# A four-layer graph network on one core: when the rows of layer 0 are gathered, released and written

## The chip, the cores and the metric

The kernel runs on one core of a Trainium2 chip. The metric is the device time of one execution in microseconds (us), lower is better; each kernel is run several times and the median counts. The engines are named as in the profile: PE is TensorE's matmul, PEld its weight load, DVE VectorE, ACT ScalarE, POOL GpSimd, SP SyncE. L849 is line 849 of the kernel before.

## The reference

A graph of 3125 nodes and 100,000 edges goes through four layers. Each layer ends in `x = layernorm(x + layer(x))`. Layer 0, the one that the change touches, is an attention over the edges that end in a node:

```python
pre_edge = hP1[dst] + hP2[src] + zP3[edge_type]          # 128 wide
logit_edge = leaky(pre_edge) @ y_w                       # 8 heads
alpha = softmax of the logits over the edges of each dst (and one self edge)
t_edge = hWh[src] + zWz[edge_type]
out = leaky(segment_sum(alpha * t_edge, dst) + residual_weight * h)
# nodes without edges keep h
```

`h` is the input x, `z` a table of 500 relations with 64 values each. Layer 1 averages the rows of the neighbours and applies two dense layers. Layer 2 is an attention with four heads and a bias from edge attributes; layer 3 an attention whose matrices depend on node type and edge type. Layers 1 to 3 use the same edges.

## The kernel before

The nodes are ordered by their number of edges and cut into 25 tiles of 128 (`NT`, `P`). A node is a partition. Tile t has CAP[t] slots, and slot s holds the s-th edge of each of its 128 nodes: 57 slots in the largest tile, 21 in the smallest, 821 in all. Eight slots (`W`) make a chunk, four a group. There are 215 groups.

At the start, tables are built in HBM: `h_tab` has, for each node, the 264 values of the source's part of an edge (`HC`), `z_tab` the same for a relation, with the relation's own 64 values. Layer 0 then runs over the tiles (L1026). For a tile it gathers the tile's own rows of x (`own`, L799 to L803, a memset and an indirect gather, three buffers of `x`), multiplies them by the weights (`prologue`, which leaves `hw` and `hq`), and walks over the tile's chunks. The function `runs` (L70) cuts a tile into runs of at most three chunks and says of each chunk in which of two ways it is done:

- `gathered` (L851): for each slot POOL gathers 128 rows of `h_tab` into `hs` and 128 rows of `z_tab` into `zs`; DVE adds them.
- `multiplied` (L871): POOL gathers only `hs`; the relation's part comes from matmuls. SP loads the relation numbers as `rb` (L878), DVE makes one-hot matrices `oh` (L883), PE multiplies them by the table into `zps` (L892), ACT copies that to `zT` (L894), PE adds it to `pre` (L896) and into `t_ps` (L904), which DVE adds to `hs` (L905). 77 chunks are done so.

In both, PE forms `pre` for each group of four slots, ACT takes its relu as `low` (L831), and PE multiplies `low` by the heads' weights into `lg` (L835). After the relu of group g, ACT copies one value of it into `gates[g]` (L833).

`gates` holds POOL back. `held(rows, g)` (L846 to L849) lets POOL copy `gates[g - LEAD]`, with LEAD = 6, into the first partition of the rows that the following gathers fill. The copy has to wait for ACT's copy of six groups earlier, and the gathers follow it on POOL. `hs` has eight buffers, a chunk each. In `gathered` there is one such copy for each four slots; in `multiplied` one for a whole chunk, ahead of its eight gathers:

```python
hs = wp.tile([P, W, HC], F32, name="hs", bufs=8)
held(hs, g)
for s in range(n):
    gather(hs[:, s, :], h_tab, srcx[:, o + s:o + s + 1])
```

After a run, the softmax weights and the weighted sums of its chunks are put on the list `owed`, and after the last run of a tile `close` (L953) is put there too. The list is paid bit by bit (`pay_some`) between the chunks of the next run, so a tile is closed in the first run of the next tile. `close` forms the layer's output `y` (L1000, which reads the tile's `x`), its layernorm `x1` (L759 is the layernorm's last instruction), and scatters the 128 rows of `x1` to the table `x1_tab` in HBM with `put` (an indirect DMA of POOL, L106). Layer 1 loads that table.

The prologue of tile t+1 stands ahead of tile t's last chunk, `own(t + 1)` at the start of tile t. Work for later layers (counts of edges by pairs, names beginning with `c_`) is woven between the chunks by the generator `steps`.

The order of the instructions on each engine is not quite that of the source. The program is recorded and a planner writes out each engine's list by costs and due times that it assumes, with `tc.high_priority` bringing some instructions forward. So an instruction of a tile can stand on its engine among those of its neighbours: the scatter of tile 5's rows, for example, is issued by POOL during tile 7.[...]

Of the kernel before, what the change touches and what calls it, by code (L numbers as in the profile page):

```python
# [8 lines left out]
F32 = mybir.dt.float32  # L9
# [9 lines left out]
P = 128  # L19
N = 3125  # L20
NT = 25
# [7 lines left out]
D = 128  # L29
# [59 lines left out]
def tile_gnn(ctx, tc, a, out):  # L89
# [12 lines left out]
    def gather(dst, table, idx, **kw):  # L102
        return G.indirect_dma_start(out=dst, out_offset=None, in_=table, in_offset=indirect(idx), **kw)  # L103
# [373 lines left out]
    od = Order("d", order_d)  # L477
# [300 lines left out]
    with tc.tile_pool(name="l0", bufs=2) as wp, tc.tile_pool(name="l0s", bufs=1) as sp, \  # L778
# [67 lines left out]
        def held(rows, g):  # L846

            if g is not None and g >= LEAD:
                G.tensor_copy(rows[:1, :, 0], gates[:1, g - LEAD:g - LEAD + 1].to_broadcast([1, rows.shape[1]]))  # L849
# [21 lines left out]
        def multiplied(hq, o, n, zbT, first, lg_ps, g):  # L871

            hs = wp.tile([P, W, HC], F32, name="hs", bufs=8)
            held(hs, g)
            for s in range(n):
                gather(hs[:, s, :], h_tab, srcx[:, o + s:o + s + 1])
            rb = wp.tile([P, W * P], F16, name="rb")
            nc.sync.dma_start(rb[:, :n * P], rel_tab[o:o + n].rearrange("(o s) p -> o (s p)", o=1)  # L878
                              .to_broadcast([P, n * P]))
            ohs = []  # L880
            for i in range(NK):
                oh = wp.tile([P, W * P], BF16, name="oh", bufs=NK + 2)
                V.tensor_scalar(oh[:, :n * P], rb[:, :n * P], relid[:, i:i + 1], None, op0=OP.is_equal)  # L883
                ohs.append(oh)
            zT = wp.tile([P, W * P], F32, name="zT")
            for s0 in range(0, n, 4):
                k = min(4, n - s0)
                cols = slice(s0 * P, (s0 + k) * P)
                zps = ps1.tile([P, 4 * P], F32, name="zps")[:, :k * P]
                for i in range(NK):  # L890
                    for k2 in range(2):
                        T.matmul(zps, zq[:, i, 2 * R * k2:2 * R * (k2 + 1)], ohs[i][:, cols], start=(i + k2 == 0),  # L892
                                 stop=(i == NK - 1 and k2 == 1))
                A.activation(zT[:, cols], zps, AF.Copy)  # L894
                pre = argument(hq, k)
                T.matmul(pre[:, :k], zw[:, :D], zT[:, cols], start=False, stop=False)  # L896
                for s in range(k):
                    T.matmul(pre[:, s, :], hs[:, s0 + s, :D], ident, start=False, stop=(s == k - 1))  # L898
                logits(pre, k, lg_ps[:, s0:s0 + k], g + s0 // 4)
            for s0 in range(0, n, 3):  # L900
                k = min(3, n - s0)
                t_ps = ps1.tile([P, 3, HC - D], F32, name="t_ps")
                for s in range(k):
                    T.matmul(t_ps[:, s, :], zT[:, (s0 + s) * P:(s0 + s + 1) * P], zw[:, D:], start=True, stop=True)  # L904
                V.tensor_add(hs[:, s0:s0 + k, D:], hs[:, s0:s0 + k, D:], t_ps[:, :k])  # L905
            assert n == W
            zh = wp.tile([P, W // 2, P], F32, name="zh", bufs=1)
            z3 = zT.rearrange("z (s p) -> z s p", p=P)
            V.tensor_add(zh, z3[:, :W // 2], z3[:, W // 2:])
            halved(zh, W // 2, zbT if first else None)  # L910
            if not first:
                V.tensor_add(zbT, zbT, zh[:, 0])
            return hs
# [39 lines left out]
        def close(t, x, hw, ac, za, zbT):  # L953

            zaT_ps = ps1.tile([P, P], F32, name="tp", tag="misc")
            T.transpose(zaT_ps[:R], za, ident)
            zaT = wp.tile([R, P], F32, name="zaT")
            A.activation(zaT, zaT_ps[:R], AF.Copy)
            zb_ps = ps1.tile([P, 2 * D], F32, name="zb_ps", tag="misc")
            T.matmul(zb_ps, zbT, zw[:, :2 * D], start=True, stop=False)  # L960
            T.matmul(zb_ps, zaT, zw[:R, :2 * D], start=False, stop=True)
            zb = wp.tile([P, 2 * D], F32, name="zb")
            V.tensor_scalar(zb, zb_ps, od.rdeg[:, t:t + 1], None, op0=OP.mult)
            self_ = wp.tile([P, 2 * D], F32, name="self")
            V.tensor_add(self_, hw[:, D:3 * D], zb)
            V.tensor_add(self_[:, :D], self_[:, :D], hw[:, :D])
            V.scalar_tensor_tensor(self_[:, :D], self_[:, :D], 0.2, self_[:, :D], op0=OP.mult, op1=OP.max)
            sT = transposed(wp, ps1, self_[:, :D], "xT", "misc")
            sl_ps = ps1.tile([P, H], F32, name="sl_ps", tag="misc")
            T.matmul(sl_ps, sT, yw, start=True, stop=True)  # L970

            sl = wp.tile([P, H], F32, name="sl")
            V.tensor_sub(sl, sl_ps, hw[:, D + HC:])
            mf = wp.tile([P, 3, H], F32, name="mf")
            V.tensor_max(mf[:, 0, :], sl, m[:, t, :])
            V.tensor_sub(mf[:, 1, :], sl, mf[:, 0, :])
            V.tensor_sub(mf[:, 2, :], m[:, t, :], mf[:, 0, :])
            A.activation(mf[:, 1:, :], mf[:, 1:, :], AF.Exp)
            V.tensor_mul(l[:, t, :], l[:, t, :], mf[:, 2, :])
            V.tensor_add(l[:, t, :], l[:, t, :], mf[:, 1, :])  # L980
            rl = wp.tile([P, H], F32, name="rcl")
            V.reciprocal(rl, l[:, t, :])
            V.tensor_mul(mf[:, 1:, :], mf[:, 1:, :], rl.unsqueeze(1).to_broadcast([P, 2, H]))

            def heads(ap):
                return ap.rearrange("p (h d) -> p h d", h=H)

            ts = self_[:, D:]
            V.tensor_mul(heads(ac), heads(ac), mf[:, 2, :].unsqueeze(2).to_broadcast([P, H, D // H]))
            V.tensor_mul(heads(ts), heads(ts), mf[:, 1, :].unsqueeze(2).to_broadcast([P, H, D // H]))  # L990
            V.tensor_add(ac, ac, ts)
            V.scalar_tensor_tensor(ac, x, rw, ac, op0=OP.mult, op1=OP.add)
            V.scalar_tensor_tensor(ac, ac, 0.2, ac, op0=OP.mult, op1=OP.max)
            has = wp.tile([P, 2], F32, name="has")
            V.tensor_scalar(has[:, 0:1], od.deg[:, t:t + 1], 0.0, None, op0=OP.is_gt)
            V.tensor_scalar(has[:, 1:2], od.deg[:, t:t + 1], 0.0, 1.0, op0=OP.is_le, op1=OP.add)

            V.tensor_scalar(ac, ac, has[:, 0:1], None, op0=OP.mult)
            y = wp.tile([P, D], F32, name="y")
            V.scalar_tensor_tensor(y, x, has[:, 1:2], ac, op0=OP.mult, op1=OP.add)  # L1000
            x1 = wp.tile([P, D], F32, name="x1")
            layernorm(wp, x1, y, t)
            put(x1_tab, od, t, x1)

            x1T = transposed(wp, ps1, x1, "xT", "misc")
            u_ps = ps1.tile([P, D], F32, name="u_ps", tag="misc")
            T.matmul(u_ps, x1T, w1T, start=True, stop=True)
            u3 = wp.tile([P, 3, D], BF16, name="u3")
            A.activation(u3[:, 0, :], u_ps, AF.Copy)
            rest = wp.tile([P, D], F32, name="rest")  # L1010
            V.tensor_sub(rest, u_ps, u3[:, 0, :])
            V.tensor_copy(u3[:, 1, :], rest)
            V.tensor_sub(u3[:, 2, :], rest, u3[:, 1, :])
            nc.sync.dma_start(u_tab[:, t * 3 * D:(t + 1) * 3 * D], u3.rearrange("p k d -> p (k d)"))

        x1st = own(0)
        ahead = x1st, prologue(0, x1st)
        owed = []
        g = 0

        def pay_some(parts):
# [4 lines left out]
        for t in range(NT):  # L1026
            n = CAP[t]
            x, (hw, hq) = ahead
            if t + 1 < NT:
                x_next = own(t + 1)  # L1030
            ac, za, _ = sums_of(t)
            lg_ps = ps1.tile([P, max(CAP), H], F32, name="lg")
            zbT = wp.tile([P, P], F32, name="zbT")
            unset = True
            for run in runs(t):
                hss = []
                for i, (s0, w, mult) in enumerate(run):
                    o = OFF[t] + s0
                    if s0 + w == n and t + 1 < NT:

                        ahead = x_next, prologue(t + 1, x_next)
                    if mult:
                        hs = multiplied(hq, o, w, zbT, unset, lg_ps[:, s0:s0 + w], g)
                        unset = False
                    else:
                        hs = gathered(hq, lambda s: srcx[:, o + s:o + s + 1], rel[:, o:o + w], w, za,
                                      lg_ps[:, s0:s0 + w], g)
                    g += -(-w // 4)
                    hss.append((s0 - run[0][0], w, hs))
                    pay_some(len(run) - i if len(runs(t)) > 1 else max(1, len(run) - 1 - i))  # L1050

# [12 lines left out]
                    owed.append(lambda ac=ac, hs=hs, lg=lg, q=q, w=w: spread(ac, hs, lg[:, q:q + w], w))  # L1064
            owed.append(lambda t=t, x=x, hw=hw, ac=ac, za=za, zbT=zbT: close(t, x, hw, ac, za, zbT))
        pay_some(1)


    with ExitStack() as ctx1, tc.tile_pool(name="l1", bufs=2) as wp, tc.tile_pool(name="l1s", bufs=1) as sp:
# [371 lines left out]
```

## Time and profile before

| | |
|---|---|
| time, median of 3 runs | 5285.81 us (5254.62 to 5292.59) |
| profiled execution | 5243.0 us |
| its span in the profile | 5241.3 us |
| layer 0 | about 208 to 2490 us of the span |
| layer 1 | 2490 to 2620 us |
| layer 2 | 2620 to 3900 us |
| layer 3 | 3900 to 5241 us |
| PE, DVE, POOL busy | 41%, 58%, 55% of the span |

The profile is one execution; its instructions' times are measured by the chip's profiler. The borders of the layers are read from where the lines of each begin and end. Busy time is a sum over instructions of an engine. A "group" is all instructions of one line and operation: its busy time, the mean of one in ns, and the idle time of the engine just before them with the work that ended most of it. The "waits" view sums that idle time by the waiting instruction and its releaser. POOL issues the indirect DMAs[...].

### The profile page before, as it was taken

How to read it: one execution, taken by the hardware profiler on the slowest of the kernel's cores; microseconds unless marked ns; L12 is line 12 of the kernel's file. 1: busy time of each engine (PE TensorE's matmuls, PEld its weight loads, DVE VectorE, ACT ScalarE, POOL GpSimd, SP SyncE). 2: the span in 40 equal slices, each digit the busy share in tenths (PEclk: the TensorE clock that was granted, in tenths of full speed). 3: DMA queues.
4: the chain of work that ended last, by engine and by line, in shares of the span. 5: the costliest groups of instructions: out<-in, count | busy, mean ns of one | idle time of the engine just before them, and what ended most of it. 6: DMA issues, size and time to landing. Idle time of an engine off the chain costs nothing. (4 is left out here: it accounts for less than half of the span.)

```text
span 5241.3 us, 41048 instructions
## 1 busy us (share of the span) xinstructions
PE 2170.7 (41%) x12091; PEld 1405.0 (27%) x12091; DVE 3025.1 (58%) x7369; ACT 1018.4 (19%) x2777; POOL 2860.7 (55%) x3030
## 2 busy tenths in 40 slices
PE   7267676677767677777830122222232000000000
PEld 5145444455545454545310001011111000000000
DVE  8346555666656666656224576556664554454646
ACT  1023233333333333332100111111111000000000
POOL 0545444555545454453047666666663777666664
PEclk9578778778877787878865555555566555555555
DMA  3423222333323233332533333333342333233232
GB/s 82 122 80 86 80 80 80 87 99 90 99 79 87 75 90 86 82 97 75 215 106 99 99 109 106 109 105 113 104 113 73 105 96 93 79 92 94 86 92 58
DMA packets 213060, 498.45 MB, mean 95 GB/s; under 512 B 62329, under 2 KB 109100, under 8 KB 208185
## 3 DMA queue, kind: packets, MB, share of 16 engines
q0 software_dynamic: 136448, 397.65, 26.8%
q1 hardware_dynamic: 76344, 97.76, 6.0%
q8 instruction: 102, 1.67, 0.1%
q14 instruction: 166, 1.36, 0.1%
HBM read 424.65 MB, written 70.63 MB: 94 GB/s over the span
## 5 line engine op out<-in xcount | busy, mean ns | idle before, releaser
L103 POOL DMA_INDIRECT kv<-kv_tab,pay_sb x821 | 783.2, 954 | 384.9 <-issue 245.6
L103 POOL DMA_INDIRECT hs<-h_tab,srcx x821 | 848.3, 1033 | 262.0 <-issue 212.9
L103 POOL DMA_INDIRECT kv<-ktv_tab,pay_sb x821 | 802.6, 978 | 333.0 <-issue 244.2
L730 DVE TENSOR_REDUCE u<-msg 128x128 f32<-128x1024 f32 (+4 forms) x228 | 384.0, 1684 | 144.4 <-remote 94.6
L892 PE MATMUL zps<-oh,zq 128*128 128x512 bf16 x1232 | 397.4, 443 | 37.1 <-DVE oh L883 20.7
L835 PE MATMUL lg<-yw,low 128*128 128x8 f32 x1642 | 242.0, 274 | 150.0 <-ACT low L831 72.7
L849 POOL COPY hs<-gates 1x8 f32<-1x8 f32 (+3 forms) x133 | 41.2, 310 | 467.0 <-ACT gates L833 446.6
L835 PEld LDWEIGHTS lg<-yw,low 128*128 128x128 f32 x1642 | 234.5, 218 | 210.3 <-ACT low L831 100.1
L103 POOL DMA_INDIRECT zs<-z_tab,rel x205 | 213.1, 1039 | 124.7 <-issue 55.2
L623 ACT ACTIVATE c_oha<-c_oha,srclo 128x50 bf16<-128x50 bf16 (+2 forms) x821 | 206.0, 345 | 264.9 <-DVE c_oha L571 193.0
L904 PE MATMUL t_ps<-zw,zT 128*128 128x136 f32 x1232 | 225.7, 312 | 75.2 <-DVE hs L905 36.4
L905 DVE TENSOR_TENSOR hs<-hs,t_ps 128x408 f32<-128x408 f32 (+1 forms) x231 | 122.0, 528 | 227.8 <-PE t_ps L904 81.3
L726 DVE TENSOR_TENSOR msg<-kv,ex 128x1024 f32<-128x1024 f32 (+4 forms) x228 | 248.7, 1102 | 2.9 <-issue 1.8
L896 PE MATMUL pre<-zT,zw 128*128 128x512 f32 x308 | 205.7, 756 | 101.6 <-issue 62.4
L741 PE MATMUL tp<-ident,an 128*128 128x128 f32 x25 | 11.3, 453 | 560.7 <-DMA kv<-kv_tab,pay_sb 172.0
L904 PEld LDWEIGHTS t_ps<-zw,zT 128*128 128x128 f32 x1232 | 194.5, 213 | 109.7 <-issue 50.0
L898 PEld LDWEIGHTS pre<-ident,hs 128*128 128x128 f32 x1232 | 189.0, 221 | 95.3 <-issue 94.6
L824 PE MATMUL pre<-identb,hq 128*128 128x512 bf16 (+3 forms) x645 | 204.6, 417 | 5.9 <-issue 3.4
L831 ACT ACTIVATE low<-pre 128x512 f32<-128x512 f32 (+2 forms) x215 | 122.9, 574 | 400.8 <-PE pre L898 159.1
L1290 PE MATMUL xk_ps<-of,xqb 128*128 128x512 f32 x50 | 50.9, 1121 | 358.0 <-DVE xqb L759 204.9
L898 PE MATMUL pre<-ident,hs 128*128 128x128 f32 x1232 | 194.1, 306 | 0.0
L1378 DVE TENSOR_TENSOR qk<-kv,qp 128x1024 f32<-128x1024 f32 (+4 forms) x114 | 126.5, 1110 | 114.9 <-DMA kv<-ktv_tab,pay_sb 98.2
(399 smaller groups left out, 5384.6 us busy)
## 6 DMA issues: line engine op xcount, KB each, us to landing
rb<-rel_tab SPq DMA_DIRECT2D x77, 256.0 KB
c_tab<-c_sb SPq DMA_DIRECT2D x25, 768.0 KB
cs<-c_tab SPq DMA_DIRECT2D x6, 3200.0 KB
hs<-h_tab,srcx POOLq DMA_INDIRECT x821
kv<-kv_tab,pay_sb POOLq DMA_INDIRECT x821
kv<-ktv_tab,pay_sb POOLq DMA_INDIRECT x821
h_tab<-h SPq DMA_DIRECT2D x25, 132.0 KB
zs<-z_tab,rel POOLq DMA_INDIRECT x205
```

What stands on the lines that cost most here:

```text
L103: return G.indirect_dma_start(out=dst, out_offset=None, in_=table, in_offset=indirect(idx), **kw)
L623: A.activation(oha[:, s // 2, 0, :, s % 2], oha[:, s // 2, 1, :, s % 2], AF.Copy, scale=srclo[:, o:o + 1])
L726: V.tensor_tensor(msg[:, :n, :].rearrange("p s (h d) -> p s h d", h=heads), val.rearrange("p s (h d) -> p s h d", h=heads), ex.unsqueeze(3 ...
L730: V.tensor_reduce(u, msg[:, :n, :].rearrange("p s d -> p d s"), AX.X, OP.add)
L824: T.matmul(pre[:, :k], hq[:, i, :], identb.unsqueeze(1).to_broadcast([P, k, P]), start=(i == 0), stop=False)
L831: A.activation(low[:, :k], pre[:, :k], AF.Relu)
L835: T.matmul(lg_ps[:, s, :], low[:, s, :], yw8, start=True, stop=True)
L892: T.matmul(zps, zq[:, i, 2 * R * k2:2 * R * (k2 + 1)], ohs[i][:, cols], start=(i + k2 == 0), stop=(i == NK - 1 and k2 == 1))
L896: T.matmul(pre[:, :k], zw[:, :D], zT[:, cols], start=False, stop=False)
L898: T.matmul(pre[:, s, :], hs[:, s0 + s, :D], ident, start=False, stop=(s == k - 1))
L904: T.matmul(t_ps[:, s, :], zT[:, (s0 + s) * P:(s0 + s + 1) * P], zw[:, D:], start=True, stop=True)
L1378: V.tensor_mul(qk[:, :n], kv[:, :n, :D], qp.unsqueeze(1).to_broadcast([P, n, D]))
```

## The change

There are three edits, all in layer 0.

1. In `multiplied` a gate copy stands ahead of each four gathers instead of ahead of all eight. The second four wait for the gate of the next group.
2. `own(t + 1)` moves from the start of tile t to just ahead of its last chunk, beside the prologue that uses it.
3. `close` no longer scatters the tile's `x1`; it appends it to the list `finished`. After each chunk of a tile's last run `put_rows(1)` scatters what is in the list but for the newest entry, so that tile t-2's rows leave in tile t's last run. After the last tile `put_rows(0)` scatters the rest. `x1` gets three buffers.

```diff
@@ def multiplied
             hs = wp.tile([P, W, HC], F32, name="hs", bufs=8)
-            held(hs, g)
             for s in range(n):
+                if s % 4 == 0:
+                    held(hs[:, s:min(s + 4, n)], g + s // 4)
                 gather(hs[:, s, :], h_tab, srcx[:, o + s:o + s + 1])
@@ def close
-            x1 = wp.tile([P, D], F32, name="x1")
+            x1 = wp.tile([P, D], F32, name="x1", bufs=3)
             layernorm(wp, x1, y, t)
-            put(x1_tab, od, t, x1)
+            finished.append((t, x1))
@@ ahead of the loop over the tiles
-        owed = []
+        owed, finished = [], []
+
+        def put_rows(keep):
+
+            while len(finished) > keep:
+                k, rows = finished.pop(0)
+                put(x1_tab, od, k, rows)
+
@@ for t in range(NT)
             x, (hw, hq) = ahead
-            if t + 1 < NT:
-                x_next = own(t + 1)
             ac, za, _ = sums_of(t)
...
-            for run in runs(t):
+            runs_t = runs(t)
+            for run in runs_t:
                 hss = []
                 for i, (s0, w, mult) in enumerate(run):
                     o = OFF[t] + s0
                     if s0 + w == n and t + 1 < NT:
 
+                        x_next = own(t + 1)
                         ahead = x_next, prologue(t + 1, x_next)
...
                     g += -(-w // 4)
+                    if run is runs_t[-1]:
+                        put_rows(1)
                     hss.append((s0 - run[0][0], w, hs))
...
         pay_some(1)
+        put_rows(0)
```

## Prediction

> **What bounds the kernel now.** I read the busy shares first, then busy time by stage, then the waits of POOL and of PE inside layer 0, then the timeline around the waits that the change touches. The first line is the span; the second the engines' busy time; then the row of the gate copies (columns: busy, mean ns | idle time before it, and what ended most of that).
>
> ```profile
> span 5241.3 us, 41048 instructions
> ...
> PE 2170.7 (41%) x12091; PEld 1405.0 (27%) x12091; DVE 3025.1 (58%) x7369; ACT 1018.4 (19%) x2777; POOL 2860.7 (55%) x3030
> ...
> L849 POOL COPY hs<-gates 1x8 f32<-1x8 f32 (+3 forms) x133 | 41.2, 310 | 467.0 <-ACT gates L833 446.6
> ```
>
> No engine is full over the span, so I cut it by layers (columns: window, its length, busy PE, PEld, DVE, ACT, POOL, clock, DMA share, GB/s): layer 0, then layer 1, layer 2, layer 3.
>
> ```profile
> 208.00:2490.00 2282.00, 1613.89 (x9845) 1114.50 (x9844) 1382.57 (x3954) 747.17 (x2119) 1162.85 (x1231) 0.78 0.32 86
> 2490.00:2620.00 130.00, 105.23 (x440) 46.77 (x441) 33.79 (x148) 14.66 (x52) 2.77 (x1) 0.88 0.58 216
> 2620.00:3900.00 1280.00, 302.68 (x719) 139.13 (x716) 733.12 (x1596) 157.67 (x359) 811.91 (x851) 0.58 0.35 107
> 3900.00:5241.00 1341.00, 41.91 (x89) 18.50 (x87) 715.76 (x1191) 76.46 (x171) 847.81 (x867) 0.51 0.30 87
> ```
>
> The change touches layer 0 alone. There PE is busy 1613.9 of 2282 us (71%), POOL 51%: PE is nearest to a bound. What does POOL wait for in that window (total, times, longest)?
>
> ```profile
> POOL hs L849 <- ACT gates L833: 446.6, 66, 38.6
> ...
> POOL x L801 <- DVE y L1000: 139.7, 12, 18.7
> POOL x_tab L106 <- DVE x L759: 79.6, 11, 27.1
> ```
>
> The first wait is wanted: the gate keeps POOL six groups behind PE's use. The other two are what the moves aim at. Are gathers late? I took, from the trace's instructions, each gather's end and the matmul that reads its slot: the smallest distance is 25 us, the median 59. So gathers are not late, and a wait of POOL as such costs PE nothing. What costs is something else. There are stretches of layer 0 in which PE, PEld, DVE and ACT have no instruction at all while POOL gathers without a pause:
>
> ```profile
> 233.20:257.80 24.60, 0.00 (x0) 0.00 (x0) 0.00 (x0) 0.00 (x0) 18.69 (x21) 0.50 0.47 126
> 887.40:899.60 12.20, 0.00 (x0) 0.00 (x0) 0.00 (x0) 0.00 (x0) 6.87 (x8) 0.63 0.35 95
> ```
>
> I call them holds. Together the four engines stand still 318 us in layer 0, in 86 pieces over 1 us and many short ones; 243 us lie under gathers. Most end 1 to 4 us after the run of gathers ends. In the second, POOL's last gather starts at 895.46 and DVE and ACT move again from 899.70:
>
> ```profile
> 895.46 0.94 POOL L103 DMA_INDIRECT hs<-h_tab,srcx  x1 [0.30 <-issue]
> 899.70 0.26 DVE L571 TENSOR_TENSOR c_oha<-c_digb,c_up 128x200 bf16<-128x200 bf16 x1 [20.65 <-remote]
> ...
> 901.43 0.58 ACT L831 ACTIVATE low<-pre 128x512 f32<-128x512 f32 x1
> ```
>
> PE's semaphore updates for matmuls that ended from 881.8 on arrive bunched at 899.6. So long unbroken runs of gathers go with engines that hear of each other late. I counted, for each gather, how many came before it since POOL's last other instruction or pause over 1 us, with the still time of all four beside it: 1st to 4th: 572 gathers, 0.15 us each (85.7); 5th to 8th: 337, 0.353 (119.0); 9th to 12th: 113, 0.517 (58.4); later: 52, 0.914 (47.5). The sum is 310.6 us.
>
> [...]
>
> **The change part by part.**
> (1) A second gate in each of the 77 multiplied chunks. 154 of the 215 groups are in them; 76 gates are new (133 to 209; the very first chunks have none). A copy between two gathers takes 0.19 us and lengthens the pause from 0.30 to 0.45 us: 0.34 us each, 76 x 0.34 = 26 us of POOL, hidden in its 446.6 us of gate waits. The added wait: behind it on POOL's queue stand the other four gathers, then the next chunk. The gate of group g-5 opens on average 10.8 us after that of g-6 (median 6.5, 90% within 25.7); I replayed POOL's list with these times: the later four gathers move by a median of 2.5 us, 75% by at most 9.1, at most 26.5; median distance to the reader falls from 59 to 53, the smallest stays near 23. Gate waits grow by some 157 us in the replay, off the path. So by readiness of data it costs nothing. If that cover is gone, every us beyond 23 is paid by PE.
> What it can bring: no run of multiplied gathers is longer than four without another POOL instruction. If a copy alone starts the count anew, counts become 841, 135, 32, 18 (gathers and scatters of rows among them), and the still time 841 x 0.15 + 135 x 0.353 + 32 x 0.517 + 18 x 0.914 = 126 + 48 + 17 + 16 = 207, with 7 for the row transfers 214: 96 us less than 310. If only a real pause counts, the replay gives nothing (239 to 250 in its measure). A gate that makes POOL wait is a pause; one already open is only a copy. In seven places a hold ended 1 to 3 us after a copy in mid-run, some 0.7 endings per us against 0.2 elsewhere: few, but for the first reading. I take two thirds of the 96, 64: not all, as seven cases are few.
> (2) Own rows gathered at the last chunk. Memset and gather (0.20 + 1.02 us) remain, 25 of each; they pass the tile's earlier gathers on POOL, and SP is not involved. The 12 waits (139.7 us) for y of two tiles back go: y is done by then. But the gate after them is late next: in 10 of 12 POOL waits again there, as here, where 18.63 us at x are followed by 6.20 at the gate.
>
> ```profile
> 1032.79 0.20 POOL L801 MEMSET x<- 128x128 f32 x1 [18.63 <-DVE y L1000]
> 1033.61 1.02 POOL L103 DMA_INDIRECT x<-in_x,node_d  x1 [0.61 <-POOL x L801]
> 1040.83 0.18 POOL L849 COPY hs<-gates 1x4 f32<-1x4 f32 x1 [6.20 <-ACT gates L833]
> ```
>
> So it gains 0. Its cost: x comes 50 to 80 us ahead of the next prologue instead of 65 to 190; hidden, 0. It also removes pauses that break runs: bounded by 12 new holds as long as the second window, 12.2 us: 0 to +146, taken 0 because the gate pauses instead.
> (3) Scatter a tile later. 25 scatters of about 1.1 us remain. Some 32 us of in-loop waits (79.6 less 27.1 and 20.2 at the layer's end) turn into gate waits: 0. At the end the rows of the last two tiles leave back to back after the final close; the last one waits for the same x as before, and the rows of layer 1 are loaded after it: 0, at most +1.3 us for one more gather-sized issue.
> x1's third buffer keeps the next tile's layernorm from waiting: 0.
> Sum: -64 + 0 + 0. Profiled execution 5243.0 (span 5241.3) to 5179; the median of the runs is 5285.8, 43 us above the profiled one, and I carry the difference over: 5286 - 64 = 5222.
>
> **The rivals.**
> B, nothing: only real pauses end a hold, and in half the chunks the second gate is open within 6.5 us, about the time of four gathers (4 x 1.25 = 5 us). Then the copy is just 0.34 us more of POOL, and x and scatter waits become gate waits. For it: the replay; holds such as the first contain gate copies. Against: the seven endings. Time 5286, within 25.
> C, slower: the instruction lists are written by a planner, and an added POOL wait and moved x, scatter and prologue give other lists. [...]its waits for neighbours in layer 0 total 72.7 (low) + 36.4 (hs) + 34.6 (lgs) + 30.2 (zT) + 20.7 (oh) = 194.6 us:
>
> ```profile
> PE lg L835 <- ACT low L831: 72.7, 24, 10.3
> ...
> PE t_ps L904 <- DVE hs L905: 36.4, 22, 5.5
> ```
>
> If they grow by a third, +65 and no gain: 5351. It decides once this growth exceeds what the gates gain; with B's gain of nothing, from the first us, with A's 64 us, from a third. For it: the order is delicate and the gate loops POOL to ACT to PE. Against: distances stay over 22 us.
> D, the change does all it says and holds vanish to the table's end: 5286 - 96 = 5190.
>
> **How the numbers follow.** A (5222) 0.42, D 0.10, B 0.28, C 0.20. A measurement of this kernel can tell about 1%, 53 us, from no change. A's forecast is 64 us, little beyond that: 0.31 of its 0.42 lie beyond the bound, and D's 0.10: faster 0.41. B, with A's remaining 0.11: 0.39. C: 0.20. Range: from D less some 38 for the runs' own spread (5254.62 to 5292.59), 5152, to near C's time, 5340, leaving out half of C and little of D. A's own range is 5185 to 5260.
>
> **What would show it.** Gate copies 209; no x waits on y, in-loop scatter waits gone; gate waits about 600 us; layer 0's last scatter at about 2423 instead of 2487; still time 318 to about 254, with fewer pieces over 10 us; layers 1 to 3 as long as before. If the still time stays near 318, B holds; if PE's waits above grow or gathers become the releaser of PE's matmuls, C. The forecast is wrong if holds turn out to have another cause than the length of a run of gathers.

## The result, and the profile after

| | before | after |
|---|---|---|
| median | 5290.31 us (5248.22 to 5301.61, 11 runs) | 5219.61 us (5187.76 to 5224.72, 11 runs) |
| ratio | | 0.9878, 95% interval 0.9854 to 0.9901 |
| span of the profiled execution | 5241.3 us | 5219.9 us |
| last scatter of layer 0 ends | 2488.4 us | 2441.6 us |
| rest of the span | 2752.9 us | 2778.3 us |

The change makes the kernel 1.2% faster: 71 us between the medians, where 64 were forecast. The size was right; the experiments below show that part of the reasoning was not. The experiments ran in four sets, each on one chip together with the kernel before, and that kernel ran at two quite different speeds: it took 4382 and 4384 us in the first two sets, and 5233 and 5273 in the last two. Every ratio below is taken against runs of the kernel before in the same set.

The page of the changed kernel, its first line and the row of the gate copies:

```profile
span 5219.9 us, 41130 instructions
...
L849 POOL COPY hs<-gates 1x4 f32<-1x4 f32 (+2 forms) x209 | 55.9, 269 | 442.8 <-ACT gates L833 432.1
```

There are 209 copies instead of 133, as counted. The cut by layers (window, length, busy PE, PEld, DVE, ACT, POOL, clock, DMA share, GB/s), with borders where this execution has them:

```profile
208.00:2443.00 2235.00, 1599.71 (x9713) 1115.65 (x9844) 1385.20 (x3953) 746.43 (x2119) 1186.89 (x1308) 0.79 0.32 88
2443.00:2573.00 130.00, 103.70 (x426) 46.28 (x436) 33.65 (x147) 14.07 (x50) 2.77 (x1) 0.87 0.58 216
2573.00:3885.00 1312.00, 313.24 (x720) 141.72 (x721) 741.09 (x1623) 160.12 (x366) 822.93 (x864) 0.57 0.35 106
3885.00:5219.00 1334.00, 45.47 (x87) 19.39 (x87) 705.86 (x1166) 74.27 (x166) 835.62 (x854) 0.51 0.30 86
```

Layer 0 is 47 us shorter (2282 to 2235), and no engine works less for it (PE's line lacks 132 matmul records): ACT 747.2 to 746.4, DVE 1382.6 to 1385.2, POOL more by the copies. So waiting went. What follows layer 0, in which no line changed, is 25 us longer in this pair of executions. The medians are 71 us apart, the two profiled executions 21 us: the one of before (5243.0 us) was quicker than all eleven runs of the table. Which part of the 71 us lies outside layer 0 can't be told from one profile of each.

The waits of POOL in layer 0 after (total, times, longest):

```profile
POOL hs L849 <- ACT gates L833: 432.1, 86, 29.0
...
POOL x L801 <- DVE y L1001: 130.7, 10, 19.5
POOL x_tab L106 <- DVE x L759: 70.4, 10, 28.2
```

Here the prediction's picture breaks. The waits for y were to vanish, and 130.7 of 139.7 us are still there; so are those of the scatters, 70.4 of 79.6. The timeline of POOL shows why, in tile 14:

```profile
1633.10 0.20 POOL L801 MEMSET x<- 128x128 f32 x1 [15.81 <-DVE y L1001]
1633.92 1.02 POOL L103 DMA_INDIRECT x<-in_x,node_d  x1 [0.61 <-POOL x L801]
1637.58 1.10 POOL L106 DMA_INDIRECT x_tab<-x,node_d  x1 [2.64 <-DVE x L759]
1638.69 0.18 POOL L849 COPY hs<-gates 1x4 f32<-1x4 f32 x1
```

The memset of the next tile's rows still stands at slot 7 of 31, the slot where the kernel before has it, and not at the last chunk. I compared the place of all 25 on POOL's list, counted in gathers. From tile 2 on none has moved by more than four slots; only the rows of tile 1 now come after 41 slots of tile 0 instead of at its start. All scatters stand within four slots of where they were. The scatters of a tile's rows stood two tiles later already, in the tile in which edit 3 writes them; most own rows stand neither where the source before has them nor where edit 2 writes them. Those two edits change the source and hardly the lists.

What did change is the still time, in which PE, PEld, DVE and ACT all have no instruction: 317.7 us before, 268.9 after, nearly as much less as layer 0 is shorter. The waits of PE say the same. Those with a named releaser come to 496 us before and 511 after. Those for which the trace has no releaser, called "issue", fell from 183 to 127 us. The largest such row, before and after:

```profile
PE pre L896 <- issue: 62.4, 14, 31.1
```

```profile
PE pre L897 <- issue: 27.9, 12, 4.7
```

### The profile page after: what moved, and what is told of

Read it like the earlier page. It is cut to its first block, busy times and chain, and to the rows that moved or that the text cites. A ratio compares the mean times of both kernels' runs of the same rounds, so it can differ in the third digit from the quotient of the medians.

```text
span 5219.9 us, 41130 instructions
## 1 busy us (share of the span) xinstructions
PE 2168.9 (42%) x11947; PEld 1409.2 (27%) x12091; DVE 3025.7 (58%) x7369; ACT 1017.3 (19%) x2777; POOL 2883.4 (55%) x3106
## 5 line engine op out<-in xcount | busy, mean ns | idle before, releaser
L893 PE MATMUL zps<-oh,zq 128*128 128x512 bf16 x1100 | 362.3, 443 | 51.8 <-DVE oh L884 24.8
L835 PE MATMUL lg<-yw,low 128*128 128x8 f32 x1642 | 245.9, 276 | 149.6 <-ACT low L831 73.3
L849 POOL COPY hs<-gates 1x4 f32<-1x4 f32 (+2 forms) x209 | 55.9, 269 | 442.8 <-ACT gates L833 432.1
L905 PE MATMUL t_ps<-zw,zT 128*128 128x136 f32 x1232 | 223.0, 309 | 56.9 <-DVE hs L906 35.5
L897 PE MATMUL pre<-zT,zw 128*128 128x512 f32 x308 | 208.2, 764 | 75.6 <-ACT zT L895 44.2
L899 PEld LDWEIGHTS pre<-ident,hs 128*128 128x128 f32 x1232 | 191.0, 223 | 79.6 <-issue 78.3
L884 DVE TENSOR_SCALAR oh<-rb,relid 128x1024 bf16<-128x1024 f16 x308 | 146.5, 490 | 83.5 <-PE zps L893 38.0
```

What stands on the lines that cost most here:

```text
L835: T.matmul(lg_ps[:, s, :], low[:, s, :], yw8, start=True, stop=True)
```

## The experiments

**Which edit does it.** In the first set each part ran alone, with two kernels that tell the effects of the gate apart: the copy in mid-run, and the longer wait. Edit 1 alone has the two gates of the diff above.

> Edit 1 alone: the second gate in each multiplied chunk, own rows and scatters as before. Theory A (the added gate is the whole gain): ratio to before 0.987, within 0.984 to 0.990; layer 0 (first gather of hs to the last scatter of x1) 2280 to about 2236 us, still time of the four engines about 270 instead of 318 us. Rival R (the moves bring the gain, or it needs both): within 0.5% of before, still time above 305.

Edits 2 and 3 alone keep the single `held(hs, g)`.

> Edits 2 and 3 alone: own rows at the last chunk, scatter a tile later, one gate a chunk as before. The planner leaves most of the moved instructions where they were. Theory A: ratio 1.000 within 0.004, x memsets still wait for y some 10 to 12 times (130 to 140 us), layer 0 2280 us. Rival R: 0.987, or half of the gain, 0.993.

A break in the run, but earlier gates:

```diff
-            held(hs, g)
             for s in range(n):
+                if s % 4 == 0:
+                    held(hs[:, s:min(s + 4, n)], g + s // 4 - 1)
                 gather(hs[:, s, :], h_tab, srcx[:, o + s:o + s + 1])
```

> As edit 1, but both gates one group earlier: the first four gathers of a multiplied chunk behind group g-7, the last four behind g-6. So there is a copy in mid-run, but no gather waits longer than before. If the break counts: 0.988 to 0.992, still time below 285. If what counts is that gathers are held back longer: 1.000 or slower, still time above 310.

No break, but a later gate:

```diff
-            held(hs, g)
+            held(hs, g + 1)
```

> One gate for all eight gathers as before, but that of group g-5 instead of g-6: gathers held back longer, runs of eight as before. If the break counts: 1.000 within 0.004. If the holding back counts: 0.985 to 0.992, as edit 1, still time about 270.

The kernel before took 4382 us in this set, not 5290. Judged by the next set's profile (about 50 us of still time in layer 0, the kernel before at 4384 us), there was little still time to lose, and the ratios don't decide between the theories; the later gate fell outside both ranges given for it. The ratios: edit 1 alone 1.0042 (1.0029 to 1.0056), the moves alone 1.0010 (1.0003 to 1.0016), the early gates 1.0018 (1.0011 to 1.0025), the later gate 1.0066 (1.0053 to 1.0080). The moves alone behaved as the lists say, next to nothing. Each kernel with an added or a later gate lost a little, and the more the later its gates.

**Is it the set or the kernel?** So the changed kernel itself, the kernel before, and the kernel before without gates made the second set. The last differs in one line:

```diff
-LEAD = 6
+LEAD = 10000
```

> The changed kernel again, beside the kernel before on the same chip. On the chip of the first four experiments edit 1 alone cost 0.4% and the moves alone 0.1%, and the four engines' still time was only about 138 us of layer 0 instead of 318. Theory A' (what a second gate gains is the still time that it takes away; where there is hardly any, only its holding back is left): if the kernel before takes about 4380 us here, the ratio is 1.002 to 1.006; if it takes about 5290 us, 0.985 to 0.991. Rival R' (the three edits together do something that none does alone): 0.988 on either.

> The kernel before, unchanged, for its profile on this chip. Theory A': where it takes about 4380 us, PE's semaphores reach ACT within about 1 us also under long runs of gathers, still time about 138 us, gate waits of POOL about 85 us; where it takes about 5290, still time about 318 and gate waits about 450.

> The kernel before without any gate copy; POOL is held only by the eight buffers of hs. If long runs of gathers hold up the other engines on this chip: slower by 1 to 4%, with still time up by 50 us or more. If they don't: within 0.5%, and faster rather than slower (0.995 to 1.000), since nothing waits for a gate.

The kernel before took 4384 us. The changed kernel: 1.0019 (1.0010 to 1.0028), a small loss, and less than the losses of its parts in the first set together. Without gates: 1.0043 (1.0029 to 1.0057), slower where up to 0.5% faster was expected, so gates are worth something also when nothing is held up. The four engines' still time is about 50 us in layer 0 by the count of the table below, not the 138 that the expectations name.

The profile of the kernel before in this set shows what differs. Layer 0 of that execution, then POOL's wait at the gates:

```profile
204.00:1940.00 1736.00, 1430.35 (x9713) 1018.64 (x9844) 1377.18 (x3949) 742.92 (x2118) 1199.79 (x1230) 0.87 0.41 113
```

```profile
POOL hs L849 <- ACT gates L833: 91.3, 30, 13.7
```

DVE and ACT are busy for the same time as in the 5241 us execution within 1%, POOL for 3% more, and layer 0 takes 1736 instead of 2282 us. POOL waits 91 us at the gates instead of 447. PE is busy 184 us less, of which some 54 us are an estimate for the 132 matmul records that this trace lacks, at 410 ns, the mean of their line there; the clock is 0.87 instead of 0.78. Layer 1, in which POOL has one instruction, is as long as in the prediction's row for it, at about the same clock:

```profile
1940.00:2070.00 130.00, 102.75 (x421) 45.66 (x430) 33.43 (x147) 14.07 (x50) 2.77 (x1) 0.86 0.58 216
```

So the slower execution doesn't have a lower clock everywhere. The waits of ACT in layer 0 name the place. First the 5241 us execution, two of its rows in which the releaser is "remote", that is, a semaphore update without an instruction just before it that would explain it:

```profile
ACT low L831 <- remote: 125.9, 23, 11.6
ACT zT L894 <- remote: 104.0, 12, 35.6
```

Then the only such row of the 4385 us execution of the same kernel:

```profile
ACT zT L894 <- remote: 1.7, 1, 1.7
```

Over layer 0 these rows add up to 347.8 us for ACT and 302.8 for DVE in the first, and to 1.7 and 0 in the second. From the end of the last matmul of a group to ACT's relu, with ACT free, the median is 0.04 us in both; over 1 us it takes 37 times in the first (144 us in all) and once in the second. So in the first execution results of PE are heard of late. That goes with the prediction's holds (around the second, the trace has no update of PE's semaphore between 886.13 and 899.61 us, and then seven up to 899.85), and it belongs to a condition that one set has and another has not.

The traces differ in one more way. Layer 0 has some 3410 instructions of DVE that update its semaphore; the 5241 us execution has records of 2705 such updates, the 4385 us one of 3400. Of landings of DMAs they have 7511 and 20042. In layer 1 the records are complete in both (126 of 126 and 125 of 125; 680 and 692 landings). In layer 0 of the 5241 us execution the other engines lack records too: 1865 of 2073 for PE, 1067 of 1349 for ACT, 141 of 156 for POOL. Whether the updates came late and merged, or only their records were lost, isn't shown, nor whether the recording itself has a part in the delays; and some of the waits called "remote" or "issue" can be put down wrongly for it.

**The test in a set with holds.** In the third set the kernel before took 5233 us.

> Edit 1 alone once more, because two chips on which the kernel before takes about 4383 us gave another sign than the chip of the first comparison (5290 us). Theory A': if the kernel before takes about 5290 us here, 0.985 to 0.991, and layer 0 shorter by 35 to 50 us; if about 4383, 1.003 to 1.006, with the loss again in tiles 2 and 22. Rival (the move of the own rows makes tile 0 shorter and is part of the gain): on a chip of 5290 us only 0.990 to 0.995.

> Edit 1 with both gates one group earlier (g-7, g-6), once more. On a chip where the kernel before takes about 5290 us: if the break in the run counts, as the split, 0.985 to 0.992; if the holding back counts, 0.998 to 1.004. On a chip of 4383 us: 1.001 to 1.003.

The third kernel puts a copy ahead of each two slots, in `multiplied` and `gathered` alike:

```diff
-                if s % 4 == 0:
-                    held(hs[:, s:min(s + 4, n)], g + s // 4)
+                if s % 2 == 0:
+                    held(hs[:, s:min(s + 2, n)], g + s // 2 - 2)
                 gather(hs[:, s, :], h_tab, srcx[:, o + s:o + s + 1])
```

> The changed kernel with a gate copy ahead of each two slots in both kinds of chunk (groups g-8, g-7, g-6, g-5 for the four pairs), so that no gather waits longer than in the changed kernel and more runs are cut, with some 200 more copies at 0.34 us of POOL. On a chip of 5290 us: if breaks count, 0.97 to 0.985; if not, 0.985 to 0.992 as the changed kernel or worse. On a chip of 4383 us, where there are no holds to end: 1.000 to 1.006.

Edit 1 alone: 0.9898 (0.9851 to 0.9946), the whole of the change within the intervals. The early gates: 0.9976 (0.9955 to 0.9997), a quarter of it, between the two ranges given for them, and the two intervals just don't meet. The fine gates: 0.9821 (0.9769 to 0.9874). The rows of the gate copies in the three profiles, in this order:

```profile
L849 POOL COPY hs<-gates 1x4 f32<-1x4 f32 (+2 forms) x209 | 58.5, 282 | 418.6 <-ACT gates L833 406.8
```

```profile
L849 POOL COPY hs<-gates 1x4 f32<-1x4 f32 (+3 forms) x208 | 52.9, 263 | 421.6 <-ACT gates L833 387.2
```

```profile
L849 POOL COPY hs<-gates 1x2 f32<-1x2 f32 (+1 forms) x404 | 104.4, 279 | 393.3 <-ACT gates L833 347.1
```

The first two have as many copies (209, 208); they differ in how often a copy made POOL wait. The waits view gives it for each:

```profile
POOL hs L849 <- ACT gates L833: 406.8, 83, 29.0
```

```profile
POOL hs L849 <- ACT gates L833: 387.2, 66, 37.5
```

With the split 83 copies wait; with the early gates 66, the number of the kernel before; with the fine gates 82. PE's "issue" waits in layer 0 are 98, 190 and 150 us, against 183 in the kernel before: so these two counts part the early gates from the two kernels that gain. The windows of layer 0, split, early and fine:

```profile
207.00:2412.00 2205.00, 1603.91 (x9845) 1111.96 (x9844) 1382.70 (x3951) 747.01 (x2119) 1193.56 (x1306) 0.80 0.32 89
```

```profile
208.00:2453.00 2245.00, 1608.28 (x9845) 1107.72 (x9844) 1382.62 (x3949) 745.85 (x2118) 1178.88 (x1305) 0.79 0.31 88
```

```profile
205.00:2400.00 2195.00, 1595.85 (x9844) 1101.30 (x9843) 1381.77 (x3951) 744.98 (x2118) 1221.88 (x1504) 0.80 0.32 90
```

So I counted again, and let only a pause of over 1.5 us between two gathers start the count anew; copies don't. Still time beside a gather, in us each, the pause after it included:

| gather since the last pause | before | after | early | fine | before, in the 4384 us set |
|---|---|---|---|---|---|
| 1st to 4th | 0.015 (x348) | 0.019 (x408) | 0.017 (x367) | 0.008 (x422) | 0.034 (x142) |
| 5th to 8th | 0.195 (x252) | 0.146 (x262) | 0.133 (x248) | 0.179 (x251) | 0.015 (x119) |
| 9th to 12th | 0.283 (x155) | 0.299 (x171) | 0.398 (x171) | 0.382 (x159) | 0.034 (x97) |
| 13th to 16th | 0.462 (x103) | 0.515 (x115) | 0.344 (x91) | 0.438 (x107) | 0.087 (x88) |
| 17th to 20th | 0.421 (x70) | 0.545 (x58) | 0.323 (x64) | 0.422 (x63) | 0.066 (x88) |
| later | 0.927 (x146) | 1.109 (x60) | 0.890 (x132) | 0.787 (x71) | 0.046 (x536) |

Counted so, the first four gathers after a pause have almost no still time in any kernel, and the rates of the four kernels with holds lie close together. What differs is how many gathers come late in a run without a pause: 146, 60, 132, 71. In the last column, without holds, a gather costs 0.02 to 0.09 us wherever it stands, though 536 of them stand 21st or later. With the rates of before and the counts of after, the sum is 6 + 51 + 48 + 53 + 24 + 56 = 239 us, measured 254; before has 311. So a run of gathers did no harm by itself there; under the condition of the slower sets still time goes with its length without a real pause. That this length is the cause isn't shown: the counts come from one profile of each kernel, and those of before and after are not from the set of early and fine, in which the kernel before has no profile and ran 58 us faster (medians 5232.74 and 5290.31).

This count doesn't order everything. The split alone has 109 late gathers and less still time (240) than its counts and the rates of before give (284). And a gate that makes POOL wait both breaks a run and holds the following gathers back. The kernel of the first set that holds back without a break, the later gate, wasn't run in a set with holds, so the two are not told apart there.

**A tighter and the same fine gate.** In the last set the kernel before took 5273 us, on the chip with the number of the first set, where it took 4382 us: so the holds are not a property of one chip. The tighter kernel is the fine one with LEAD = 5.

> The kernel with a gate copy ahead of each two slots, all gates one group later (g-7, g-6, g-5, g-4 for the four pairs). If what shortens the holds is that POOL really stands still between gathers, and gathers stay early enough: on a chip where the kernel before takes about 5240 to 5290 us at most as long as the looser one beside it (ratio 0.970 to 0.982); if the last pair comes too late: 0.985 or more, with PE waiting for hs. On a chip of 4383 us: 1.004 to 1.012.

> The kernel with a gate copy ahead of each two slots (g-8 to g-5) again, in five rounds. On a chip of 5240 to 5290 us: 0.978 to 0.987, again faster than the changed kernel's 0.988. On a chip of 4383 us, where hardly any hold is to be ended: 1.000 to 1.006, as the changed kernel's 1.002.

Fine: 0.9873 (0.9826 to 0.9920). Tight: 0.9900 (0.9867 to 0.9932). The fine gates beat the kernel before in both sets, but the second ratio, just above the range expected, is that of the changed kernel, so they can't be called better than it. The tighter gates bring nothing more, though POOL waits longer at them (385.2 us in the fine kernel beside it): holding gathers back one group further brings no gain there. In the tighter kernel, the waits of POOL at the gates, and a wait of PE between 205 and 2400 us:

```profile
POOL hs L849 <- ACT gates L833: 478.0, 91, 22.5
```

```profile
PE pre L897 <- ACT zT L895: 80.7, 34, 15.8
```

It has only 66 late gathers, and still its layer 0 took 2243 us: the still time went down no further (265 by the same count), and PE's wait for zT was 80.7 us there, against 61.1 in the fine kernel beside it. Gathers are not too late: all but the first five and the last two end over 20 us ahead of their matmul.

## Why the prediction was right or wrong

- **The size and the sign**: -64 forecast, -71 measured between the medians. That they agree so well is in part luck: the 64 rest on a count that the early gates contradict, layer 0, where all 64 were to come, is 47 us shorter in the profiles, and in two of four sets the kernel has hardly any hold to end. The layer's end came at 2442 where 2423 was forecast, the still time at 269 where 254 was; layers 1 to 3, forecast as long as before, took 25 us more in the profiled pair.
- **Part 1, which carried the whole gain**: right that edit 1 carries it (0.9898 alone) and that it does so in the holds. The step that failed is the count: "if a copy alone starts the count anew". With the early gates there are 75 more copies and a gain of 0.24%. Seven places where a hold ended after a copy were too few to decide it. The replay of POOL's list, which I set aside as rival B, counted by the unit that fits better, a pause, and got the wrong size (239 to 250, no gain). It took the gates' times of before as given; that this is why it missed is likely and not shown.
- **The gate's wait**: forecast to grow by 157 us in the replay, to about 600; measured 432.1, less than the 446.6 of before, in a layer 47 us shorter.
- **Parts 2 and 3, taken at 0**: right in time (1.0010 alone, in a set without holds; alone in a set with holds they weren't run, and the interval of edit 1 alone, 0.9851 to 0.9946, leaves room for some tenths of a per cent), wrong in mechanism. The waits were not turned into gate waits; they stayed, because the instructions stayed. "That the change doesn't do what it says" should have stood among the rivals: the profile of before showed the memset of tile 8 after tile 7's first run, far from its place in the source.
- **Rival C**, PE's waits for neighbours up by a third: 194.6 us before; after 73.3 (low) + 35.5 (hs) + 17.3 (lgs) + 44.2 (zT) + 24.8 (oh) = 195.1. It didn't happen there. Where nothing is held up it shows in small: edit 1 alone is 15.5 us behind the kernel before at the end of tile 2, of 19 at the end of the layer. There the wait of PE between 434 and 545 us is:

```profile
PE c_ps L649 <- DVE c_ohd L571: 15.9, 3, 11.4
```

  In the kernel before of the second set it is 3.7 us once, up to the same point of the work. So PE waits 12 us longer there for the one-hot matrices of the counts; why, no run shows.
- **"The smallest distance is 25 us"** left out the start: the fifth gather of tile 0 ends 3 us ahead of PE. After the first five, the smallest distance from the end of a gather's record to the start of its matmul is 22 us. The first stretch that I showed, 233 to 258 us, is therefore not a hold alone: without holds tile 0 has still stretches of 12.3 and 16.7 us too. Tile 0 holds 66 of the 318 us.

Open: what the condition is that makes PE's results be heard of late, and how a gather comes into it. The remote waits of ACT and DVE did not fall with the change (347.8 + 302.8 us before, 357.9 + 322.0 after). What fell is the time in which all four engines have nothing else, and PE's "issue" waits; how fewer long runs of gathers bring that about isn't shown.

## What to carry to other kernels

Before a step is priced as moved, look where its instruction stands on the engine's list in the profile: with a planner in between, the list may keep its own place for it whatever the source says, and the edit is nearly void. A copy that doesn't wait and a copy that waits are two different things (209 copies with 83 waits gave 0.9898 here, 208 with 66 gave 0.9976); count the waits, not the instructions. And a gain that comes from a condition of the machine should be measured where the condition is absent too: here the same edit is worth 1.2% in one and costs 0.2% in the other.

## What the runs showed of the hardware

The same program takes 4384 or 5273 us in different sets, 20% apart, with nearly the same busy times of DVE and ACT in layer 0. The slower execution has 650.6 us of waits whose releaser the trace calls remote in layer 0, for ACT and DVE together, the faster one 1.7. It isn't confined to layer 0: from the first to the last gather from kv_tab, layer 2 takes 1221 us in the 5241 us execution and 1059 in the 4385 us one, and layer 3's gathers from ktv_tab take 1181 and 1057. Together with layer 0 these make some 830 of the 856 us between the two. But the stretch between layers 0 and 2, from the last scatter of layer 0 to POOL's next indirect DMA, takes 180 and 182 us. So the two conditions differ where POOL issues indirect DMAs, and there the slower one also has fewer records of semaphore updates (2705 against 3400 for DVE in layer 0). In the slower condition, the engines' still time lies beside gathers from about the fifth after a pause on (0.2 us each, 0.9 from the 21st on), and hardly beside the first four (0.015 us).
